# Edge attributes copied into tables ordered by source bucket and summed there by one-hot products, in place of scatter-adds; node stage with merged weights

## The chip, the core and the metric

The kernel runs on one core of one Trainium2 chip. The core has five instruction queues that run side by side: TensorE (PE, with its weight loads shown as PEld), VectorE (DVE), ScalarE (ACT), GpSimd (POOL) and SyncE (SP). In this kernel SP issues plain DMA transfers, and POOL issues the indirect ones, whose row addresses lie in an SBUF tile. All transfers run on the core's 16 DMA engines. The metric is the device time of one execution in microseconds; lower is better.

## What is computed

Two graph layers over 6250 nodes of 128 features and 100,000 edges, sorted by destination `dst`; `src` is random.

```python
# layer 0
radial = gaussian_smearing(edge_weight)                       # 50 values per edge
h = silu(concat(x[src], x[dst], radial) @ Wm1 + bm1)
messages = silu(h @ Wm2 + bm2) @ Wm3 + bm3
out = segment_sum(messages, dst)
u = silu(concat(x, out) @ Wu1 + bu1) @ Wu2 + bu2
x = layernorm(x + silu(u @ Wi1 + bi1) @ Wi2 + bi2)
# layer 1
xt = logmap0(x); xs = xt[src]
att = sigmoid(concat(xs, xt[dst], edge_attr_128) @ att_w.T + att_b)
agg = segment_sum(xs * att, src)
mean_src = segment_sum(edge_attr_128, src) / max(count(src), 1)
mean_dst = segment_sum(edge_attr_128, dst) / max(count(dst), 1)
x = layernorm(x + proj(expmap0(xt + agg + mean_src + mean_dst)))
```

The change is about `segment_sum(edge_attr_128, src)`: 100,000 rows of 512 bytes summed into 6250 rows in a random order.

## The kernel before

Edges are taken in 98 groups of 1024 (the last has 672). A group is 4 windows of 256 edges; a window holds 2 edges per partition, so a group has 8 blocks of 128 edges, numbered b = 0 to 7. Nodes are taken in 49 blocks of 128, so a node is a high part (block) and a low part (partition).

**Start.** Node projections x @ Wm1 (source half and destination half) are written to the DRAM tables `p_src` and `p_dst`; index tiles are built: `src_i`, `hif` and `lof` (high and low parts), `rel` (destination within its window's 64 nodes). Transposed x goes to DRAM as `x_t`.

**Edge loop** (lines 1058 to 1086, 98 + 2 passes of two halves). The order on every engine is that of the program. Per group: POOL gathers 8 blocks of `p_src` rows two groups ahead (`gather`, line 932, into `ga`); SP loads the broadcast source numbers `rows_all` (line 902) and destination numbers and distances `near`, the attributes `attr`, and 4 slices of `p_dst` (`load_rows`). PE forms layer 1 (`pa`, lines 999 and 1002: transposes of `ga`, features times `lw`), layer 2 (`pb`) and the sums over destinations with one-hots (`ps`, lines 1032 to 1036); ACT does the silu. DVE adds `ps` into the SBUF accumulator `acc` (line 1048). DVE also makes the target row of each edge: `seen` (line 948) compares the block's 128 sources with each other and counts equal ones before each edge; that `rank` times the table height plus the node's row is `to_i` (line 966). So two edges of one block never have the same target row.

**The scatter-adds** (line 868). Each block's 128 attribute rows go from SBUF to a DRAM table by an indirect DMA with add. There are three tables `t_src`, each of three layers (`RK`) for equal sources in one block, used in turn, since a scatter must wait for the one before it in its table. They are filled with zeros early in the edge loop (line 1070). From group 3 on, blocks 0 and 1 go in the edge loop. All other blocks wait: `scatter_late` loads three windows again (`attr_late`, four buffers) and scatters 6 blocks. 18 such portions are called in the node stage, 74 in the attention loop, the rest behind it.

**Node stage** (lines 1149 to 1189), 13 batches of up to 4 node blocks: xT is read back from `x_t`; `acc` holds the transposed message sums, attribute sums and counts; PE forms `po` = Wm3 part, `pu` = Wu1 parts, `pv` = Wu2, `pw` = Wi1, `py` = Wi2 plus bias plus x. Then a layernorm over all blocks (line 1140) and three reductions (lines 1200 and 1201), and the small steps of logmap0.

**Attention loop** (lines 1243 to 1281), one pass a group. SP loads `los` (low parts of source and destination, broadcast to all partitions); DVE makes the one-hots `ohT` (line 1249), `hi`, `lo` (line 1261, one for each of 8 blocks); PE looks up the two logit parts with 48 products (`pg`, line 1269), DVE picks and reduces (lines 1272, 1273), ACT takes the sigmoid; PE sums weights and counts by source with `lo` and `at` (`pS`, line 1281). SP and POOL run in program order here: each pass calls `scatter_late` ahead of its los loads.

**Closing stage** (from line 1290): the nine table layers are loaded in 7 parts and added (line 1321), divided by counts, added to `sup`, then expmap0, proj, the last layernorm and the output.

A flag `bad` is computed on the way; if an input does not fit the windows or the layers, a slower general path runs afterwards.

Of the kernel before, what the change touches and what calls it, by code (L numbers as in the profile page):

```python
# [16 lines left out]
P = 128  # L17
# [507 lines left out]

W = 64
WE = 256
RK = 3
NT = 3
NOW = 1  # L530

N_NODE, N_ATT = 18, 74

LAG = 3

# [41 lines left out]
def window_path(ctx, tc, bad, x, src, dst, edge_attr, edge_weight, Wm1, bm1, Wm2, bm2, Wm3, bm3,  # L577
# [8 lines left out]
    RROWS = ROWS + P  # L586
# [19 lines left out]
    t_src = [dram.tile([RK * RROWS, F], F32, name=f"t_src{i}") for i in range(NT)]  # L606
    x_t = dram.tile([F, NB, P], F32, name="x_t")
# [10 lines left out]
    nc.vector.tensor_scalar(dump, part, float(RK * RROWS - P), None, op0=OP.add)  # L618
# [13 lines left out]
    before = const.tile([P, P], BF16, name="before")  # L632
    nc.vector.tensor_scalar(before, cols, part, None, op0=OP.is_lt)
# [66 lines left out]
    bm3r = row(bm3, "bm3r")  # L700
    bi2r = row(bi2, "bi2r")
# [8 lines left out]
    src_i = keep.tile([P, 8, NG], I32, name="src_i")  # L710
    src_f = keep.tile([P, 8, NG], F32, name="src_f")
    row_f = keep.tile([P, 8, NG], F32, name="row_f")
    rel = keep.tile([P, 8, NG], F32, name="rel")
# [3 lines left out]
    rank_max = keep.tile([P, 8], F32, name="rank_max")  # L717
    ew3 = keep.tile([P, 8, NG], F32, name="ew3")
    nodeid = keep.tile([P, 4, NG], F32, name="nodeid")
# [3 lines left out]
    nc.vector.memset(rank_max, 0.0)  # L723
# [3 lines left out]
    zrow = const.tile([P, 5 * F], F32, name="zrow")  # L727
    nc.vector.memset(zrow, 0.0)

    def fills(t):  # L730

        return [(t[r * RROWS:r * RROWS + ROWS].rearrange("(p i r) f -> i p (r f)", p=P, i=10)[i], zrow)
                for r in range(RK) for i in range(10)]

    with tc.tile_pool(name="init", bufs=1) as init, \
            tc.tile_pool(name="initx", bufs=7) as initx, \
# [7 lines left out]
        for lo in range(0, NB, 7):  # L744
            hi = min(lo + 7, NB)
            x_sb = initx.tile([P, 7, F], F32, name="x_sb")
            full = min(hi, NFULL) - lo
            if hi > NFULL:
                nc.vector.memset(x_sb[:, NFULL - lo], 0.0)
            nc.sync.dma_start(x_sb[:, :full],  # L750
                              x[lo * P:(lo + full) * P].rearrange("(b p) f -> p b f", p=P))
            if hi > NFULL:
                nc.sync.dma_start(x_sb[:NREM, NFULL - lo], x[NFULL * P:])
            x_sbs.append(x_sb)
# [10 lines left out]
        for lo in range(0, NB, 7):  # L765
            hi = min(lo + 7, NB)
            x_sb = x_sbs[lo // 7]
            for b0 in range(lo, hi, 4):
# [6 lines left out]
                nc.scalar.dma_start(x_t[:, b0:b0 + nb], xT[:, :nb])  # L775
# [52 lines left out]
        nc.vector.tensor_copy(src_f, src_i)  # L828
# [7 lines left out]
        nc.vector.tensor_scalar(row_f, lof, float(ROWS // P), None, op0=OP.mult)  # L836
        nc.vector.tensor_add(row_f, row_f, hif[:, 0])
# [7 lines left out]
        b3 = split3(init, bm2x, [P, F], "bm2s")  # L845
        pick3 = init.tile([P, F], F32, name="pick3")
        sum3 = init.tile([P, F], F32, name="sum3")
        for i in range(3):
            is_i = init.tile([P, 1], F32, name=f"is{i}")
            nc.vector.tensor_scalar(is_i, part, float(i), None, op0=OP.is_equal)  # L850
            nc.vector.tensor_scalar(pick3 if i else sum3, b3[i], is_i, None, op0=OP.mult)
            if i:
                nc.vector.tensor_add(sum3, sum3, pick3)
        nc.vector.tensor_copy(bm2p, sum3[:, None].to_broadcast([P, 4, F]))

        nc.vector.memset(acc, 0.0)

    n_scatter = 0  # L860

    def scatter(g, b, rows_):
        nonlocal n_scatter
        t = t_src[0]
        if b >= 2 * NOW or g < LAG:
            n_scatter += 1
            t = t_src[n_scatter % NT]
        nc.gpsimd.indirect_dma_start(  # L868
            out=t[:, :], out_offset=bass.IndirectOffsetOnAxis(ap=to_i[:, b, g:g + 1], axis=0),
            in_=rows_, in_offset=None, compute_op=OP.add)  # L870
# [5 lines left out]
    with tc.tile_pool(name="eload", bufs=2) as eload, \  # L876
            tc.tile_pool(name="eattr", bufs=3) as eattr, \
# [4 lines left out]
            tc.tile_pool(name="ep3", bufs=2, space=PSUM) as ep3, \  # L882
            tc.manual_schedule():
        gas, attrs, ids, feats, hots, hid1, hid2, sums = ({} for _ in range(8))
# [7 lines left out]
        def load(g):  # L892
            nk, nf, ne = extent(g)
            e0 = g * GE
            rows = eload.tile([P, GE], I32, name="rows_all")
            near = eload.tile([P, GE], F32, name="near")
            near_i = near.bitcast(I32)
            if nf < nk:
                nc.vector.memset(rows, -1)
                nc.vector.memset(near_i[:KR], -1)  # L900
                nc.vector.memset(near[KR:], 0.0)
            nc.sync.dma_start(rows[:, :ne], src[e0:e0 + ne].partition_broadcast(P))
            nc.sync.dma_start(near_i[:KR, :ne], dst[e0:e0 + ne].partition_broadcast(KR))
            nc.sync.dma_start(near[KR:, :ne], edge_weight[e0:e0 + ne].partition_broadcast(KR))
            ids[g] = rows, near

        def load_attr(g):
            nk, nf, ne = extent(g)
            e0 = g * GE
            attr = eattr.tile([P, 4, 2, F], F32, name="attr")  # L910
            if nf < nk:
                nc.vector.memset(attr[:, nf], 0.0)
                nc.sync.dma_start(attr[:LP, nf],
                                  edge_attr[e0 + nf * WE:e0 + ne].rearrange("(p c) f -> p c f", c=2))
            nc.sync.dma_start(attr[:, :nf], edge_attr[e0:e0 + nf * WE].rearrange(
                "(k p c) f -> p k c f", k=nf, c=2))
# [19 lines left out]
        def prepare(g, half):  # L936

            nk = windows(g)
            rows, near = ids[g]
            if half == 0:  # L940
                feats[g] = (ework.tile([P, 4, 2, P], F32, name="feat"),
                            ework.tile([P, 8], F32, name="rank"))
            feat, rank = feats[g]

            seen = ework.tile([P, P], BF16, name="seen", bufs=1)
            by_block = rows.rearrange("p (k j c) -> p k c j", k=4, c=2)
            for b in range(4 * half, min(4 * half + 4, 2 * nk)):
                nc.vector.scalar_tensor_tensor(  # L948
                    seen, by_block[:, b // 2, b % 2], src_f[:, b, g:g + 1], before,
                    op0=OP.is_equal, op1=OP.mult, accum_out=rank[:, b:b + 1])  # L950
# [6 lines left out]
            if half == 0:  # L957
# [3 lines left out]
            to = ework.tile([P, 8], F32, name="to")  # L961
            nc.vector.tensor_tensor(rank_max[:, :2 * nk], rank_max[:, :2 * nk], rank[:, :2 * nk],
                                    op=OP.max)
            nc.vector.scalar_tensor_tensor(to[:, :2 * nk], rank[:, :2 * nk], float(RROWS),
                                           row_f[:, :2 * nk, g], op0=OP.mult, op1=OP.add)
            nc.vector.tensor_scalar(to_i[:, :2 * nk, g], to[:, :2 * nk], dump, None, op0=OP.min)
            del ids[g]

# [12 lines left out]
        def weigh(g):  # L981
            n = 2 * windows(g)
            prod = ework.tile([P, 8, F], F32, name="prod", bufs=1)
            nc.vector.tensor_mul(prod[:, :n], attrs[g].rearrange("p k c f -> p (k c) f")[:, :n],
                                 attw[:, 2:3].to_broadcast([P, n, F]))
# [7 lines left out]
        def layer1(i):  # L993
# [7 lines left out]
            for k in range(kk):  # L1001
                nc.tensor.matmul(pa[:, 2 * k:2 * k + 2], lhsT=lws[(4 * g + k0 + k) % NL],  # L1002
                                 rhs=feats[g][0][:, k0 + k], start=False, stop=k == kk - 1)
# [16 lines left out]
        def sum_up(i):  # L1020
# [5 lines left out]
            at_b = attrs[g].rearrange("p k c f -> p (k c) f")  # L1026
            ps = ep3.tile([P, 2, 3, W], F32, name="ps")
            for k in range(kk):
                for c in range(2):
# [4 lines left out]
                    nc.tensor.matmul(ps[:, k, 1], lhsT=at_b[:, b], rhs=hot[:, b],  # L1034
# [15 lines left out]
        clear = [f for t in t_src for f in fills(t)]  # L1050
# [6 lines left out]
        prepare(0, 0)  # L1057
        prepare(0, 1)
        for g in range(NG + 2):
            for half in range(2):  # L1060
# [7 lines left out]
                n_clear = 30 * RK // 3 // (2 * LAG) if g < LAG else 1  # L1068
# [4 lines left out]
                if LAG <= g < NG:  # L1073
                    for b in range(NOW * half, NOW * half + NOW):
                        scatter(g, b, attrs[g][:, b // 2, b % 2])
# [5 lines left out]
                if g + 1 < NG:  # L1081
                    prepare(g + 1, half)
                if g < NG and half == 1:
# [312 lines left out]
```

## Time and profile before

| What | us |
|---|---|
| 12 runs: median (lowest to highest) | 2935.99 (2920.3 to 2958.59) |
| profiled execution: its time | 2931.21 |
| its span on the core | 2929.4 |

| Engine | busy us | share of the span |
|---|---|---|
| POOL | 2058.7 | 70% |
| DVE | 1804.5 | 62% |
| PE | 1675.4 | 57% |
| PE weight loads | 1393.0 | 48% |
| ACT | 923.1 | 32% |

The mean granted PE clock was 0.705 of full speed. The DMA engines read 344.78 MB from HBM and wrote 94.11 MB. A busy share is a mean over stages that differ; the stages are told apart by their lines in the trace: `ga` runs only in the edge loop, `pu` and `pw` in the node stage, `pg` in the attention loop, `fb` in the closing stage.

### The profile page before, as it was taken

How to read it: one execution, taken by the hardware profiler on the slowest of the kernel's cores; microseconds unless marked ns; L12 is line 12 of the kernel's file. 1: busy time of each engine (PE TensorE's matmuls, PEld its weight loads, DVE VectorE, ACT ScalarE, POOL GpSimd, SP SyncE). 2: the span in 40 equal slices, each digit the busy share in tenths (PEclk: the TensorE clock that was granted, in tenths of full speed). 3: DMA queues.
4: the chain of work that ended last, by engine and by line, in shares of the span. 5: the costliest groups of instructions: out<-in, count | busy, mean ns of one | idle time of the engine just before them, and what ended most of it. 6: DMA issues, size and time to landing. Idle time of an engine off the chain costs nothing. (4 is left out here: it accounts for less than half of the span.)

```text
span 2929.4 us, 42152 instructions
## 1 busy us (share of the span) xinstructions
PE 1675.4 (57%) x13478; PEld 1393.0 (48%) x13478; DVE 1804.5 (62%) x5965; ACT 923.1 (32%) x1330; POOL 2058.7 (70%) x1590
## 2 busy tenths in 40 slices
PE   3677777776777787777776791454443444431000
PEld 2566666666666676666663451443332333331000
DVE  5565556565565655555551128998776777773267
ACT  1455555555555555555540000111000000100013
POOL 1567777777777777777777881777777777878810
PEclk8788888888888888898887786555555555555555
DMA  5987777766666676666655550676666666665484
GB/s 158 280 253 199 205 202 192 203 172 161 161 163 162 164 168 163 163 156 167 156 144 74 87 87 9 139 149 117 122 123 124 122 123 123 128 121 99 49 280 168
DMA packets 371430, 441.86 MB, mean 151 GB/s; under 512 B 46375, under 2 KB 285916, under 8 KB 371200
## 3 DMA queue, kind: packets, MB, share of 16 engines
q1 hardware_dynamic: 230216, 331.18, 37.9%
q0 software_dynamic: 138208, 103.35, 26.1%
q10 hardware_dynamic: 2776, 4.55, 0.4%
q8 instruction: 110, 1.80, 0.3%
q14 instruction: 120, 0.98, 0.1%
HBM read 344.78 MB, written 94.11 MB: 150 GB/s over the span
## 5 line engine op out<-in xcount | busy, mean ns | idle before, releaser
L868 POOL DMA_INDIRECT t_src<-attr_late,to_i x592 | 949.9, 1605 | 299.5 <-issue 159.7
L932 POOL DMA_INDIRECT ga<-p_src,src_i x782 | 787.1, 1006 | 314.8 <-issue 217.7
L1269 PE MATMUL pg<-a,ohT 128*128 128x49 bf16 x4692 | 213.4, 219 | 466.5 <-DVE ohT L1249 402.5
L1048 DVE TENSOR_TENSOR acc<-acc,ps 128x192 f32 x391 | 138.7, 355 | 542.0 <-PE ps L1036 500.9
L1269 PEld LDWEIGHTS <-ohT 128*128 128x128 bf16 x4692 | 200.4, 120 | 502.6 <-DVE ohT L1249 437.9
L999 PE MATMUL pa<-ident,ga 128*128 128x128 f32 x782 | 198.3, 335 | 345.6 <-DMA ga<-p_src,src_i 325.6
L868 POOL DMA_INDIRECT t_src<-attr,to_i x190 | 311.1, 1637 | 119.8 <-issue 66.4
L1032 PE MATMUL ps<-hot,h 128*128 128x64 f32 x1564 | 320.0, 288 | 1.4 <-ACT h L1018 1.4
L1034 PE MATMUL ps<-hot,attr 128*128 128x64 f32 x1564 | 311.6, 282 | 0.0
L999 PEld LDWEIGHTS pa<-ident,ga 128*128 128x128 f32 x782 | 105.8, 150 | 404.6 <-DMA ga<-p_src,src_i 228.6
L948 DVE SCALAR_TENSOR_TENSOR seen<-rows_all,src_f,before 128x128 bf16<-128x128 int32 x782 | 275.2, 352 | 36.1 <-DMA rows_all<-in_src_dram 12.6
L1005 ACT ACTIVATE h<-pa,bm1c 128x512 f32<-128x512 f32 x196 | 134.5, 686 | 508.9 <-PE pa L1002 508.7
L1016 PEld LDWEIGHTS pb<-wm,h 128*128 128x128 f32 x1564 | 268.4, 242 | 47.5 <-issue 23.5
L1002 PE MATMUL pa<-feat,lw 128*128 128x256 f32 x782 | 275.2, 489 | 8.2 <-DMA lw<-p_dst 8.1
L1276 ACT ACTIVATE lg<-lg,attb 128x8 f32<-128x8 f32 x98 | 29.5, 301 | 791.4 <-DVE lg L1275 791.4
L1016 PE MATMUL pb<-wm,h 128*128 128x128 f32 x1564 | 260.7, 322 | 0.0
L1032 PEld LDWEIGHTS ps<-hot,h 128*128 128x128 f32 x1564 | 251.6, 202 | 1.6 <-ACT h L1005 1.6
L1034 PEld LDWEIGHTS ps<-hot,attr 128*128 128x128 f32 x1564 | 247.6, 200 | 0.0
L1281 PE MATMUL pS<-at,lo 128*128 128x196 bf16 x782 | 145.1, 366 | 153.2 <-DVE at L1278 153.2
L1249 DVE TENSOR_SCALAR ohT<-los,part 128x2048 bf16<-128x2048 bf16 x98 | 76.2, 777 | 207.1 <-DMA los<-row_lo 207.1
L1002 PEld LDWEIGHTS pa<-feat,lw 128*128 128x128 f32 x782 | 174.1, 246 | 29.1 <-issue 8.8
L1281 PEld LDWEIGHTS <-lo 128*128 128x128 bf16 x782 | 101.0, 140 | 174.2 <-DVE at L1278 167.0
(225 smaller groups left out, 3216.8 us busy)
## 6 DMA issues: line engine op xcount, KB each, us to landing
los<-row_lo SPq DMA_DIRECT2D x196, 256.0 KB
rows_all<-in_src_dram SPq DMA_DIRECT2D x97, 512.0 KB
attr<-in_edge_attr_dram SPq DMA_DIRECT2D x97, 512.0 KB
attr_late<-in_edge_attr_dram SPq DMA_DIRECT2D x97, 384.0 KB
t_src<-zrow SPq DMA_DIRECT2D x90, 320.0 KB
fb<-t_src SPq DMA_DIRECT2D x56, 448.0 KB
near<-in_dst_dram SPq DMA_DIRECT2D x97, 256.0 KB
near<-in_edge_weight_dram SPq DMA_DIRECT2D x97, 256.0 KB
```

The source lines that it names most:

```text
L868: nc.gpsimd.indirect_dma_start(out=t[:, :], out_offset=bass.IndirectOffsetOnAxis(ap=to_i[:, b, g:g + 1], axis=0), in_=rows_, in_offset=Non ...
L932: nc.gpsimd.indirect_dma_start(out=gas[g][:, b], out_offset=None, in_=p_src[:, :], in_offset=bass.IndirectOffsetOnAxis(ap=src_i[:, b, g:g ...
L948: nc.vector.scalar_tensor_tensor(seen, by_block[:, b // 2, b % 2], src_f[:, b, g:g + 1], before, op0=OP.is_equal, op1=OP.mult, accum_out=r ...
L999: nc.tensor.matmul(pa[:, j], lhsT=gas[g][:, 2 * k0 + j], rhs=ident, is_transpose=True, start=j == 0, stop=False)
L1002: nc.tensor.matmul(pa[:, 2 * k:2 * k + 2], lhsT=lws[(4 * g + k0 + k) % NL], rhs=feats[g][0][:, k0 + k], start=False, stop=k == kk - 1)
L1005: nc.scalar.activation(hid1[i][:, :2 * kk], pa[:, :2 * kk], AF.Silu, bias=bm1c)
L1016: nc.tensor.matmul(pb[:, j], lhsT=h1[:, j], rhs=wm2, start=False, stop=j == nb - 1)
L1032: nc.tensor.matmul(ps[:, k, 0], lhsT=h2[:, 2 * k + c], rhs=hot[:, b], start=k == 0 and c == 0, stop=False)
L1034: nc.tensor.matmul(ps[:, k, 1], lhsT=at_b[:, b], rhs=hot[:, b], start=False, stop=False)
L1048: nc.vector.tensor_add(acc[:, :, bass.ds(at, W)], acc[:, :, bass.ds(at, W)], ps[:, k])
L1269: nc.tensor.matmul(pg[:, i, s], lhsT=ohT[:, s, b0 + i], rhs=a3[q][:, s], start=q == 0, stop=q == 2)
L1281: nc.tensor.matmul(pS, lhsT=lo[:, b], rhs=at[:, b], start=g == 0 and b == 0, stop=g == NG - 1 and b == n - 1)
```

## The change

The attribute rows are no longer added in DRAM. They are copied, without add, into tables in which each node block (bucket) owns a run of `cap` rows, and each edge gets a row of its own there. A row has 132 numbers instead of 128: the attributes, a one (for the count), the edge's attention weight (for blocks 3 to 7), and the low part of the source. Later each bucket's rows are loaded again, a one-hot is made of the low parts, and one product sums attributes, counts and weights of the 128 nodes.

- There are 14 tables: one lane for each of blocks 0 to 3, each split at group 70; one lane for blocks 4 and 5 and one for 6 and 7, each split at groups 35 and 70. Caps are 256 or 128 rows a bucket. Rows from a floor (`lo`) up to the cap are zeroed early in the edge loop, in 116 transfers.
- The row within the bucket comes from running counts. `rank` (PE, seven bf16 products with a triangle `tri` and `ones_b`) and `place` (DVE) take the place of `seen` and the `rows_all` load. Counts over a cap or under a floor set the flag of the general path.
- Blocks 0 and 1 still go in the edge loop from group 3 on. All blocks 2 and the six left of groups 0 to 2 go in the node stage, in 27 batches of up to 4 scatters with one load each into four buffers `r_tiles`; all blocks 2 of groups 0 to 69 go to one table, those of 70 to 97 to a second. Blocks 3 to 7 go in the attention loop, 5 a group, with their weight.
- Node stage: Wm3 Wu1b and Wu2 Wi1 are multiplied once at the start (`w3u`, `w2i`), which drops `po` and `pv` and their copies from each batch; x is loaded again and transposed, not read from `x_t`. The layernorm statistics and the two dot products are taken batch by batch, and the scaling of x is done on ACT inside the attention loop.
- Attention loop: software-pipelined by hand with los loaded three groups ahead, all engines in program order; `lo` and `at` only for blocks 0 to 2; each pass also sums one unit of buckets: 9 products (first 49 passes), 8, or 12.
- Closing stage: the last generation of lanes 3, 4/5 and 6/7 is summed in 28 units, and expmap0, layernorm and output run in 7 parts.

```diff
-RK = 3
-NT = 3
-NOW = 1
-N_NODE, N_ATT = 18, 74
+RW = 132
+EARLY, MIDDLE, LATE = (0, 1), (2,), (3, 4, 5, 6, 7)
 LAG = 3
+CUT1, CUT2 = 35, 70
+LANES = [((b,), ((0, CUT2, 256, 96), (CUT2, None, 128, 28))) for b in range(4)] + \
+    [((b, b + 1), ((0, CUT1, 256, 96), (CUT1, CUT2, 256, 96), (CUT2, None, 256, 76))) for b in (4, 6)]
...
     def scatter(g, b, rows_):
-        nonlocal n_scatter
-        t = t_src[0]
-        if b >= 2 * NOW or g < LAG:
-            n_scatter += 1
-            t = t_src[n_scatter % NT]
+        t, _ = table_of(g, b)
         nc.gpsimd.indirect_dma_start(
             out=t[:, :], out_offset=bass.IndirectOffsetOnAxis(ap=to_i[:, b, g:g + 1], axis=0),
-            in_=rows_, in_offset=None, compute_op=OP.add)
+            in_=rows_, in_offset=None)
...
-                nc.vector.scalar_tensor_tensor(
-                    seen, by_block[:, b // 2, b % 2], src_f[:, b, g:g + 1], before,
-                    op0=OP.is_equal, op1=OP.mult, accum_out=rank[:, b:b + 1])
+        def rank(g):
...
+            nc.tensor.matmul(part_(0, 0), lhsT=tri, rhs=hi[:, :4], start=True, stop=False)
+            nc.tensor.matmul(part_(0, 1), lhsT=ones_b, rhs=hi[:, :4], start=False, stop=True)
...
+        def place(g):
...
+            nc.vector.tensor_add(by_bank, counts, both(0))
+            nc.vector.tensor_add(counts, counts, both(1))
+            nc.vector.tensor_mul(prod, prod, his.pop(g))
+            slot = ework.tile([P, 8], F32, name="slot")
+            nc.vector.tensor_reduce(slot, prod, AX.X, OP.add)
...
+    middle = [[(g, b) for g in range(g0, min(g0 + 2, LAG)) for b in EARLY] for g0 in range(0, LAG, 2)]
+    middle += [[(g, b) for g in range(g0, min(g0 + 4, NG))] for b in MIDDLE for g0 in range(0, NG, 4)]
+    def move_middle():
...
+        for i, (g, b) in enumerate(bs):
+            nc.scalar.copy(t[:, i, F + 2:F + 3], lof[:, b, g:g + 1])
+        for i, (g, b) in enumerate(bs):
+            scatter(g, b, t[:, i])
...
+            nc.tensor.matmul(pu[:, :nb], lhsT=w3u, rhs=acc[:, 0, sl], start=True, stop=False)
+            nc.tensor.matmul(pu[:, :nb], lhsT=b3u, rhs=acc[:1, 2, sl], start=False, stop=False)
+            nc.tensor.matmul(pu[:, :nb], lhsT=wu1a, rhs=xT[:, :nb], start=False, stop=True)
...
+        def bucket_hot(unit, loaded):
...
+            for h in range(nh):
                 nc.vector.tensor_tensor(
+                    oh[:, h, :nj], cols[:, None, :].to_broadcast([P, nj, P]),
+                    bt[:, h, :nj, F + 2, None].to_broadcast([P, nj, P]), op=OP.is_equal)
+        def bucket_mm(unit, loaded, oh):
...
+                    nc.tensor.matmul(pb[:, h], lhsT=oh[:, h, j], rhs=bt[:, h, j, :S],
+                                     start=j == 0 and h == 0,
+                                     stop=j == nj - 1 and h == nh - 1)
...
+            def move(g):
+                t = rows_.pop(g)
+                for b in sorted(range(NE, 2 * windows(g)), key=lambda b: (b > 3 and b % 2, b)):
+                    scatter(g, b, t[:, b - NE])
...
+            for it in range(NG + 2):
...
+                one_hots(it + 1)
+                if it < NG:
+                    logits(it)
+                    move(it)
+                us = todo.get(it - 1, [])
+                pbs[it - 1] = [bucket_mm(u, l, o) for u, l, o in
+                               zip(us, loaded.pop(it - 1, []), ohs.pop(it - 1, []))]
+                look_up(it + 1)
+                if 0 < it <= NG:
+                    lo_at = weigh_one_hots(it - 1)
+                    sum_up(it - 1, *lo_at)
```

## The prediction

> **What bounds the kernel now.** I read first the busy times by stretch, cut where the chain of waits changes its line: start to first gather (77 us), edge loop (to 1546), node stage (to 1829), attention loop (to 2676), scatters left over (to 2797), closing stage. Columns: stretch, its length, busy us of PE, PEld, DVE, ACT, POOL, then the granted PE clock, DMA share, GB/s.
>
> ```profile
> 77.00:1546.00 1469.00, 1111.47 (x7289) 970.68 (x7287) 860.01 (x2964) 774.20 (x884) 1096.47 (x971) 0.85 0.71 181
> 1546.00:1829.00 283.00, 175.58 (x584) 96.43 (x583) 106.25 (x266) 20.26 (x30) 187.14 (x122) 0.72 0.44 66
> 1829.00:2676.00 847.00, 354.08 (x5424) 297.98 (x5424) 671.88 (x2342) 81.00 (x196) 661.74 (x413) 0.50 0.64 125
> 2676.00:2797.00 121.00, 4.85 (x52) 3.41 (x52) 23.09 (x90) 1.04 (x3) 102.32 (x60) 0.50 0.45 58
> 2797.00:2929.40 132.40, 0.00 (x0) 0.00 (x0) 105.75 (x241) 35.20 (x205) 0.35 (x1) 0.50 0.69 244
> ```
>
> No engine looks full, so next the costliest groups and the list of who waited for whom, for what the idle time is.
>
> ```profile
> L868 POOL DMA_INDIRECT t_src<-attr_late,to_i x592 | 949.9, 1605 | 299.5 <-issue 159.7
> L932 POOL DMA_INDIRECT ga<-p_src,src_i x782 | 787.1, 1006 | 314.8 <-issue 217.7
> L868 POOL DMA_INDIRECT t_src<-attr,to_i x190 | 311.1, 1637 | 119.8 <-issue 66.4
> ...
> PE pa L999 <- DMA ga<-p_src,src_i: 325.6, 209, 5.7
> ...
> DVE ohT L1249 <- DMA los<-row_lo: 207.1, 41, 38.2
> ...
> POOL t_src L868 <- DMA t_src<-attr_late,to_i: 74.8, 67, 2.8
> ```
>
> The idle time ahead of POOL's own instructions is mostly "issue": 0.30 us between any two of them (the timeline of POOL shows that gap at nearly every one). A group of the edge loop issues 8 gathers and 2 scatters: 8 x (1.006 + 0.30) + 2 x (1.637 + 0.30) = 14.3 us, and a group takes (1528 - 77) / 98 = 14.8 us (1528 is the start of the last gather). So POOL sets the edge loop, and PE waits 325.6 us for gathers. In the attention loop DVE waits for los, whose load stands in SP's queue behind attr_late loads that wait until scatters have freed a buffer: POOL starts 413 instructions in 847 us, one in 2.05, and some 60 more scatters at 1.55 + 0.30 fill the 121 us behind the loop. POOL bounds nearly everything up to 2797.
>
> Last, the chain of waits, for how long a scatter takes to land, counted from its start (two quiet ones, two under load):
>
> ```profile
> 1716.94 3.38 DMA t_src<-attr_late,to_i
> 2793.95 3.24 DMA t_src<-attr_late,to_i
> 2097.79 7.34 DMA t_src<-attr_late,to_i
> 2123.89 5.47 DMA t_src<-attr_late,to_i
> ```
>
> **The change part by part.** The sum is made against the profiled execution: 2931.2 us, 2929.4 of them span, 4.8 below the median shown (2936).
>
> *Scatter without add.* 782 scatters stay, of 528 instead of 512 bytes a row. No plain scatter is in the trace. Its POOL time lies between the indirect gather's 1.006 us (also 128 rows, one address a row, no add) and the adding scatter's 1.6; I take 1.0, since what it loses is the add and what it keeps is the gather's work turned round. Its landing: the quiet 3.3 us hold 1.55 us of POOL; with 1.0 instead, 2.7. With the 0.3 of issue the next dependent scatter starts 3.0 us after it; the far end is 3.3 + 0.3 = 3.6 quiet, and under load the chain's 5.5 and over.
>
> *Edge loop.* POOL per group falls to 8 x 1.31 + 2 x 1.30 = 13.1 us; gathers after one another show 0.95 in the timeline, so 12.6 at best. PE next: 1111 / 98 = 11.3 us busy now. Seven bf16 products of 98 or 196 columns are added for the rank; by the bf16 rows of 64 columns (195 ns) and 512 (495 ns) they are 0.22 to 0.28 us each, 1.8 us, and since PE's rows here overlap (the seven large groups make 1615 us against 1111 busy) 1.2 us on the path: 12.5. DVE: eight compares `seen` (0.352 us) with the small ones behind them go, one 392-wide compare, four 392-wide passes (0.55 each) and small ones come; 8.8 us a group before and after, covered. rows_all (512 KB a group) leaves SP's queue; one load for attr more and 116 fills instead of 90 enter it, under a DMA share of 0.71. I take 13.3 us a group, between 12.9 and, with the dear scatter, 14.4 (14.8 less the 38 us in which POOL's scatters and gathers waited for t_src). End of the gathers 77 + 98 x 13.3 = 1380, end of the loop 27 us behind it as now: 1407.
>
> *Middle scatters.* Here the change adds a wait. All blocks 2 go to one table (a second from group 70), so each of these 98 scatters waits until the one before it has landed; before, three tables took turns, and only 67 of 592 late ones waited. Queued behind the waiting scatter on POOL are all the others; behind the loads on SP, which wait for four buffers, stand xn and then los. 98 x 3.0 = 294, with six of blocks 0 and 1 and the first load 14 more: 308 us. Bounds: 98 x 2.65 (3.24 - 1.54 + 0.95, the issue gap running under the landing) and 98 x 3.6. The node stage's own work is hidden under it: now it ends with 54 us of layernorm and products (1774 to 1828) that move into the loop or to ACT, and two of its products a batch go; some 200 us remain. If the chain were short, these 200 would stand in its place.
>
> The Trainium skill, "DMA: Bandwidth & Descriptors", section "Anatomy of one DMA — SWDGE (gpsimd) path", speaks against such a chain: it fits 2.0 us + bytes / 436e3 to a transfer and puts most of it down to the write receipt, worst in HBM. For 67.6 KB my estimate from it is 2.2 us behind 1.0 of POOL, 3.5 with the issue; the total would be 50 us higher.
>
> *Attention loop.* Per group, 5 scatters: tables 3, 4, 5, 4, 5. Two dependent landings a group bound it: 2 x 3.0 = 6.0 quiet, 2 x 5.5 = 11 loaded. DVE: 671.9 / 98 = 6.86 us now; five compares `lo` (0.227 each by busy time) and 3 x 0.26 for the narrower `at` go: 4.95. Added is one one-hot of 1152 (the 1024-wide product costs 1.22, so 1.36), later 2 x 512 (0.69 each) or 2 x 768 (0.95), with an add of 0.43: 6.3 to 7.3. PE: 3.6 now, 2.7 without five sums; bucket products 9, 8 or 12 a group, at 0.43 us (the chain shows 0.42 for a 128x128 f32 pair in the node stage): 6.6, 6.1, 7.9. SP issues 12 DMAs instead of 3, some 5 us, covered. Three engines near 7 and a landing that varies: I take 7.9, with bounds 7.2 and 9.2, plus 10 us of ramp: 784.
>
> The clock rule of the page "TensorE: Matmul & The Clock Gate", Part 1, has the throttle let go when PE is busy; the rows agree (0.72 granted in the node stage, 0.50 here at 42% busy). By the rule the busier PE would leave 3.5 us a group; the sum is unchanged, since DVE and landings stay.
>
> *End.* The 121 us of scatters left over vanish: all are issued by the last group. Of the 132 us of closing, the 63 table loads and the 56 adds (61 us) go. Added are 28 units in 7 parts. DVE: 105.8 - 61 + 49 x 0.82 for one-hots 640 wide (between 0.69 for 512 and 0.95 for 768) + 28 x 0.4 for adds + 14 x 1.09 for two more passes a part + 14 for small steps done 7 times = 125. PE beside it: 245 x 0.43 = 105. With the sqrt, tanh, sqrt turns of the last part (3 x 1.28 of table loads and what they wait for), first load and output, 25: 150, bounds 135 (half of that covered) and 190 (the turns of all parts bare, 7 x 6 more).
>
> Sum: 1407 + 308 + 784 + 150 = 2649; with 2 us around the span 2651 in the profiled execution, 2655 beside the median.
>
> **The rivals.** *The plain scatter costs POOL as much as the adding one* (1.6). For: the same instruction with 128 addresses; against: the gather has these too. Edge 14.4 x 98 + 104 (77 ahead, 27 behind) = 1515, middle 98 x 3.6 + 14 = 367, attention 5 x 1.9 = 9.5 a group, 941, end 150: 2973 + 2, so 2975.
>
> *The landing takes the place of POOL.* Place: 98 middle scatters and 2 x 98 in the attention loop. With t from start to start the total is 1407 + 14 + 10 + 150 + 294 t + 2, above 2931 from t = 4.6 us. At 5.5, the loaded landing, it is 3200. For: the chain shows 5.5 to 7.3 there, and rows of 528 bytes lie off the old boundaries. Against: those rows are picked because they were late; one read of the old value falls away; scatters three apart (5.55 us) waited in one case of nine.
>
> *The edge loop gains nothing*, because PE, with the rank put in, or another wait keeps 14.6: 2655 + 98 x 1.3 = 2780.
>
> *The change doesn't do what it says*: with a bucket over its cap or under its floor the general path would run behind, and the time more than double. The inputs give 45 to 94 and 145 to 219 rows a bucket and table of one lane, 114 to 215 of two, within all bounds.
>
> **How the numbers follow.** Forecast 62%; edge loop without gain 15%; dear scatter 12%; landings 9%, of which over half lie above 4.6; general path 0.5%; the rest others. Predicted time 2655. Its own terms, each at the low end (12.9; 2.65; 7.2; 135), give 2500; 2900 takes in the second case, most of the attention loop at 9.2, and part of the first. What a measurement can't tell from no change is 0.3%, 9 us. Slower: the dear scatter nearly whole and most of the landings, 0.14; same 0.03; faster 0.83.
>
> **What would show it.** Right: POOL's scatter rows at 1.0 us; a group of the edge loop at 13.3; POOL in the middle idle between scatters with t_0_67 as releaser, 3.0 us from start to start; the attention loop with DVE over 80% busy at 7.9; nothing on POOL behind the last group. Wrong: scatter rows at 1.6; the middle over 400 us; an attention group over 9; a closing stage over 200.

## The result

| | median us | lowest to highest | runs |
|---|---|---|---|
| before | 2931.69 | 2917.86 to 2958.59 | 49 |
| after | 2963.0 | 2956.77 to 2970.62 | 12 |

The ratio is 1.0104, with a 95% interval of 1.0084 to 1.0123: the change costs 1%, where 2655 us was forecast, with 2900 as the far end of the range. The profiled execution of the changed kernel has a span of 2957.4 us. First its busy times by stretch, cut as those of before (stretch, length, busy us of PE, PEld, DVE, ACT, POOL, then granted PE clock, DMA share, GB/s): start to first gather, edge loop, node stage, attention loop, closing stage.

```profile
0.00:100.00 100.00, 40.76 (x179) 32.78 (x179) 50.77 (x113) 13.87 (x15) 11.26 (x26) 0.77 0.43 121
100.00:1395.00 1295.00, 1057.61 (x7944) 928.77 (x7942) 889.77 (x2207) 767.87 (x993) 975.69 (x974) 0.91 0.68 182
1395.00:1725.00 330.00, 101.87 (x488) 59.47 (x487) 76.09 (x243) 43.55 (x140) 102.40 (x105) 0.63 0.19 57
1725.00:2795.00 1070.00, 575.18 (x6623) 539.99 (x6623) 703.30 (x1993) 82.32 (x381) 501.81 (x474) 0.70 0.56 165
2795.00:2957.00 162.00, 90.11 (x621) 86.94 (x621) 130.96 (x426) 55.53 (x236) 12.08 (x11) 0.74 0.44 128
```

The edge loop is shorter: from the start of the first gather to the end of the last it takes 1279 us instead of 1438 (the 1469 of the stretch above begin before the first gather). The 121 us of scatters left over are gone. The attention loop, which now holds all its scatters, has grown from 847 to 1070, the node stage from 283 to 330. The last scatter ends at 2814.1, so 19 us of the last stretch still belong to the loop; behind it stand 143 us, where it was 132. In the attention loop no engine is near full: DVE 703 of 1070, PE 575, POOL 502. So the loop waits. The list of who waited for whom (engine and line, what it waited for: us in total, times, longest), over the whole span:

```profile
ACT attr L1466 <- DMA t<-attr,to_i: 793.4, 74, 30.5
PE pS L1530 <- DVE at L1524: 434.2, 96, 8.4
...
DVE lg L704 <- ACT att L1510: 327.7, 90, 5.9
...
ACT attr_last L1466 <- DMA t<-attr_last,to_i: 237.4, 23, 12.7
POOL t L927 <- ACT att L1510: 215.0, 89, 4.3
...
POOL t L927 <- DMA t<-attr,to_i: 203.0, 119, 4.2
```

Idle time of ACT alone would cost nothing. But here the three other engines wait in turn: PE for DVE, DVE for ACT's sigmoid (L1510), POOL for the same sigmoid, and ACT for landings of scatters ahead of L1466. The chain of waits of the changed kernel over one group (start, us, what) shows that this is a ring, a chain of waits in which each step waits for the one before it and the first for the last. (A scatter has landed when what waits for its data or its buffer may go on; the time of a landing is counted from the scatter's start on POOL.)

```profile
2270.18 0.30 ACT attr L1508
2270.48 0.19 ACT att L1510
...
2270.75 0.30 POOL t L927
2271.05 0.97 issue
2272.03 4.81 DMA t<-attr,to_i
...
2277.10 0.43 POOL t L927
2277.53 0.84 issue
2278.37 2.40 DMA t<-attr,to_i
...
2280.87 0.04 ACT attr L1466
...
2280.97 0.30 ACT attr L1508
```

Two sigmoids (L1508, L1510) free the group's five scatters. The second (block 4, 2272.03) lands 4.81 us later; block 5 goes to the same table and had to wait for it (2277.10). The last (block 7) lands 2.40 us after its start. Then ACT makes a 0.20 us copy (L1466) and the sigmoids of the next group: 10.8 us from sigmoid to sigmoid here, median 11.1 over the loop. L1466 writes the low parts of the group three ahead into the row buffer that the last group's scatters have just left (four buffers in turn), so it waits for their landing, and it stands in ACT's in-order queue ahead of the sigmoids of the present group.

One more fact is needed to read the runs below: in three of the five sets of runs PE was held back (granted clock 0.71 to 0.74 in the edge loop instead of 0.84 to 0.91), which lengthens the edge loop of every kernel, so times are compared within a set, or between sets in which PE was free.

### The profile page after: what moved, and what is told of

The parts are those of the page before. It is cut to its first block, busy times and chain, and to the rows that moved or that the text cites. A ratio compares the mean times of both kernels' runs of the same rounds, so it can differ in the third digit from the quotient of the medians.

```text
span 2957.4 us, 48129 instructions
## 1 busy us (share of the span) xinstructions
PE 1865.5 (63%) x15852; PEld 1647.9 (56%) x15852; DVE 1850.9 (63%) x4978; ACT 963.1 (33%) x1765; POOL 1603.2 (54%) x1590
## 5 line engine op out<-in xcount | busy, mean ns | idle before, releaser
L927 POOL DMA_INDIRECT t<-attr,to_i x448 | 467.5, 1044 | 623.3 <-DMA t<-attr,to_i 201.4
L1423 PE MATMUL pb<-acc,oh 128*128 128x130 f32 x2352 | 479.8, 390 | 116.1 <-issue 75.4
L1423 PEld LDWEIGHTS pb<-acc,oh 128*128 128x128 f32 x2352 | 456.0, 299 | 143.1 <-issue 103.3
L1493 PE MATMUL pg<-a,ohT 128*128 128x49 bf16 x4692 | 158.8, 194 | 218.6 <-DVE ohT L1473 206.3
L1530 PEld LDWEIGHTS <-lo 128*128 128x128 bf16 x294 | 30.5, 114 | 441.3 <-issue 432.4
L1466 ACT COPY attr<-lof 128x5 f32<-128x5 f32 x74 | 14.8, 200 | 793.4 <-DMA t<-attr,to_i 793.4
L704 DVE CAST lg<-att 128x3 bf16<-128x3 f32 x294 | 53.3, 181 | 334.4 <-ACT att L1510 327.7
L927 POOL DMA_INDIRECT t<-attr_last,to_i x144 | 150.7, 1046 | 185.2 <-DMA t<-attr_last,to_i 64.2
L927 POOL DMA_INDIRECT t<-attr_row,to_i x190 | 197.2, 1038 | 70.8 <-issue 49.4
L1139 PE MATMUL ps<-hot,attr 128*128 128x64 f32 x1172 | 227.8, 276 | 0.0
L1412 DVE TENSOR_TENSOR oh<-cols,acc 128x1152 f32<-128x1152 f32 (+3 forms) x196 | 180.9, 948 | 23.3 <-DMA acc<-t 23.3
```

The source lines that it names most:

```text
L927: nc.gpsimd.indirect_dma_start(out=t[:, :], out_offset=bass.IndirectOffsetOnAxis(ap=to_i[:, b, g:g + 1], axis=0), in_=rows_, in_offset=None)
L1139: nc.tensor.matmul(ps[:, k, 1], lhsT=head[:, b, :F] if b < 2 else rest[:, b - 2], rhs=hot[:, b], start=False, stop=False)
L1412: nc.vector.tensor_tensor(oh[:, h, :nj], cols[:, None, :].to_broadcast([P, nj, P]), bt[:, h, :nj, F + 2, None].to_broadcast([P, nj, P]), o ...
L1423: nc.tensor.matmul(pb[:, h], lhsT=oh[:, h, j], rhs=bt[:, h, j, :S], start=j == 0 and h == 0, stop=j == nj - 1 and h == nh - 1)
L1493: nc.tensor.matmul(pg[:, i, s], lhsT=ohT[:, s, b0 + i], rhs=a3[q][:, s], start=q == 0, stop=q == 2)
L1530: nc.tensor.matmul(pS, lhsT=lo[:, b], rhs=at[:, b], start=g == 0 and b == 0, stop=g == NG - 1 and b == NE - 1)
```

## The experiments

A "group" is the time from the first scatter of the attention loop to the end of the last, over 98. With PE held back the kernel before takes 3096 to 3135 us; with PE free 2931 to 2935. A set is a number of kernels run together with the kernel before (the expectations say "call"): first e1, e2, e3 and e4; then c0_after, f0, f1 and f2; then b0_before, r1, f4 and f3; then f0, f1, f2 and the kernel before again; last c0_after_c and f2. PE was held back in the first, second and fourth. The changed kernel itself, the control, ran in the second and the last.

### Controls: the changed kernel and the kernel before, as they are

> The changed kernel itself, as the control of this call, since chips differ (the one of the first call ran the kernel before in 3134 us, not in 2932). On a chip like the first: 2963, 10.9 us a group in the attention loop. On one like that of the first call: the edge loop 18.6 us a group, which no theory here speaks of, and 3440 to 3480.

> The changed kernel, as control. PE free (before near 2935): 2963, edge loop 13.0 us a group, attention 11.1. PE held back (before 3095 to 3135): 3480 to 3540, 18.5 and 11.1.

> The kernel before, as it is, for its trace on these chips, where it takes 3135 us instead of 2932 and the changed one 3537 instead of 2963. If the granted PE clock is what differs: the edge loop at a clock of 0.74 or less, PE with idle pieces that nothing ends, some 16.5 to 17 us a group instead of 14.55 (200 us in 98 groups), all other stages within 15 us of the first trace. If it is the transfers: the same clock as in the first trace, and longer landings in every stage.

> The kernel before. On a chip where it takes 2935: the trace of the first. On one where it takes 3135: the edge loop at a granted clock of 0.74 or less and 16.5 to 17 us a group, other stages unchanged, if the clock is the cause; longer landings everywhere, if the transfers are.

| run | PE | time us | edge loop, us a group | attention, us a group | behind the last scatter |
|---|---|---|---|---|---|
| c0_after | held back | 3536.5 | 18.4 | 11.1 | 143 |
| c0_after_c | free | 2967.6 | 13.1 | 11.1 | 143 |
| b0_before | free | 2940.4 | 14.7 | | 133 |
| b0_before_b | held back | 3113.3 | 16.5 | | 132 |

The attention loop does not care whether PE is held back; 11.1 belongs to the ring. The edge loop does, and the expectation of 16.5 to 17 for the kernel before held.

### Moving the copy

e1: the copy becomes `mark`, issued behind the sigmoids. e2: the copy stays, but rows are loaded two groups ahead, so that copy and load wait for the scatters of the group before last. f0 does both. In the expectations of the first set, theory A, where named, is the copy's ring; what its rivals expect stands beside it.

```diff
 # f0_copy (e1 has mark(it + 3) and load_late(it + 3); e2 changes load_late alone)
-                nc.scalar.copy(t[:, :n - NE, F + 2], lof[:, NE:n, g])
+            def mark(g):
+                if g < NG:
+                    nc.scalar.copy(rows_[g][:, :2 * windows(g) - NE, F + 2], lof[:, NE:2 * windows(g), g])
...
-                    load_late(it + 3)
+                load_late(it + 2)
...
                     logits(it)
+                    mark(it + 2)
                     move(it)
```

> Only the place of one small ACT copy in the attention loop changes: the copy that writes the low parts into the rows of group it+3 is issued behind the two sigmoids of group it instead of ahead of them. Theory A (the copy closes a loop: it waits until the scatters of group it-1 have landed, since they read the same buffer, and the sigmoid of group it, which the next scatters need, stands behind it on ACT): a group falls from 10.9 us to about 8.3, the time from 2963 to about 2710 (2660 to 2780). Theory B (two dependent landings a group on tables 4/5 and 6/7 bound the loop by themselves): a group stays above 10.5 us, 2920 to 2965. Theory C (PE with its bucket products bounds the loop): also unchanged.

> Rows are loaded and marked two groups ahead instead of three, with the same four buffers and the copy where it was, so the copy for group it+2 waits for the scatters of group it-2, not it-1. Theory A: the loop opens as in the run with the copy moved, 2690 to 2800. Theory B and C: unchanged, 2920 to 2965, or slower if the shorter look-ahead bares the loads.

> The copy of the low parts stands behind the sigmoids, and loads run two groups ahead instead of three, so that the copy waits for the scatters of two groups ago. The copy theory alone: the attention loop goes to the 7.9 us a group of the prediction, 290 us below the control. The theory of two dependent landings on one table alone: no gain, 10.9. Both: 8.9 to 9.4 a group, 150 to 200 below the control, with POOL waiting for its own landings.

> Copy behind the sigmoids alone. If PE was no limit to it on the other chip: 9.3 to 9.5 a group as there, and on a chip where before takes 2935, 2963 - 98 x 1.7 = 2795. If PE was: 8 to 8.5 a group, 2670 to 2720.

Measured, all with PE held back: e1 9.5 us a group (3360.6 us, ratio to before 1.0715, 1.0665 to 1.0765), e2 9.0 (3334.2; 1.0642, 1.0566 to 1.0719), f0 9.4 and in the repeat 9.3 (3348.5 and 3331.6). The times expected for e1 and e2 are for PE free, so there only the us a group compare. f0 lies 188 us below the control of its set. The ring through ACT is open: in the middle of the loop the sigmoid starts some 6 us ahead of its group's first scatter in e1 and e2 and 16 in f0 (medians), where in the changed kernel it starts 0.6 ahead. But the loop goes to 9.0 to 9.5, neither to the 8.3 that theory A expected of e1 nor to the 7.9 of the prediction: f0's reading "both". What holds it then, in the chain of waits of e1:

```profile
2608.10 0.98 POOL t L927
2609.09 0.33 issue
...
2609.65 5.27 DMA t<-attr,to_i
2614.92 0.27 issue
2615.18 0.96 POOL t L927
...
2618.59 5.56 DMA t<-attr,to_i
```

No ACT line is left in it: scatter, landing, next scatter of that table. In the repeat of f0 the median from the start of block 4 to that of block 5 is 4.0 us, from there to the next group's block 4 another 5.1: two dependent landings a group, 9.2 us from group to group. f0 was run with PE held back alone; since its sigmoids run far ahead of the scatters, PE is not what its scatters wait for.

### Another order, and four tables

e3 keeps the copy and turns the scatters from 3, 4, 6, 5, 7 to 4, 6, 3, 5, 7. f1 keeps the copy and gives blocks 4, 5, 6 and 7 a table each (128 rows a bucket, as many rows read back, and three products of `rank` fewer).

```diff
 # e3_order
-                for b in sorted(range(NE, 2 * windows(g)), key=lambda b: (b > 3 and b % 2, b)):
+                for b in sorted(range(NE, 2 * windows(g)), key=lambda b: (b % 2 and (1 if b == 3 else 2), b)):
 # f1_split
-    [((b, b + 1), ((0, CUT1, 256, 96), (CUT1, CUT2, 256, 96), (CUT2, None, 256, 76))) for b in (4, 6)]
+    [((b,), ((0, CUT1, 128, 48), (CUT1, CUT2, 128, 48), (CUT2, None, 128, 28))) for b in range(4, 8)]
```

> Only the order of the five scatters of a group changes, from blocks 3, 4, 6, 5, 7 to 4, 6, 3, 5, 7; the copy stays ahead of the sigmoid. Theory A: the first scatter of the pair on table 4/5 starts one issue (1.27 us) earlier in the closed loop, so a group falls by about 1.3 us: 2963 - 125 = 2840 (2810 to 2870). Theory B: two landings a group stay two landings a group, 2945 to 2970. Theory C: unchanged.

> Blocks 4, 5, 6 and 7 go to four tables instead of two, so that no scatter of a group waits for another of the same group; the rows read back stay as many. The copy theory alone: the loop sigmoid, five scatters, last landing, copy stays, 0.5 + 5 x 1.3 + 3 to 4 = 10 to 11 us a group, within 60 us of the control. The table theory alone: 7.9 a group, 290 us below.

> Four tables alone, the copy where it was: sigmoids, five scatters of 1.27, landing of the last, copy: 10.0 a group as there, 2963 - 98 x 1.1 = 2855. If PE held that run: 8 to 9 and 2660 to 2750.

e3: 10.0 a group (3420.5 us; 1.0914, 1.0867 to 1.0961). f1: 10.1 and 10.0 (3445.3, 91 below its control, and 3429.7). All three runs had PE held back. That is the copy's ring by itself, as expected for it (10 to 11 a group; the 91 us are more than the 60 expected). In f1 it is 5.9 us from the first to the last scatter and 4.1 from the last through landing, copy and sigmoid to the next group's first; in e3 6.0 and 3.8, where the changed kernel has 7.8 and 3.2: the two scatters on table 4/5, now three places apart, stretch the first part less.

### No loads of attributes in the attention loop

r1 leaves out the attribute loads of the attention loop, so old values are scattered.

```diff
-                nc.sync.dma_start(t[:, 0, :F], edge_attr[e0 + WE:e0 + 2 * WE].rearrange(
-                    "(p c) f -> p c f", c=2)[:, 1])
...
-                for k in range(2, nf):
-                    nc.sync.dma_start(t[:, 2 * k - NE:2 * k - NE + 2, :F],
-                                      edge_attr[e0 + k * WE:e0 + (k + 1) * WE].rearrange(
-                                          "(p c) f -> p c f", c=2))
```

> The changed kernel without the loads of edge attributes in the attention loop (one 128 KB and two 256 KB transfers a group; the rows scattered there hold old values), copy and tables as they are. If a loaded landing, slowed by these transfers in the same rings, is what lengthens the loop: landings near the quiet 1.9 to 2.4 us, a group at 7.4 to 8.4, DVE near full. If landings do not depend on them: within 0.5 of the control's 11.1.

2998.2 us and 11.5 a group (PE free), where the changed kernel took 2963.0 and 2967.6 in other sets: no gain, so the loads of attributes alone are not what makes the loop long. Its chain of waits:

```profile
2262.23 0.30 ACT attr_last L1503
2262.80 0.96 POOL t L927
...
2264.07 0.96 POOL t L927
...
2265.34 1.18 POOL t L927
...
2266.82 1.31 POOL t L927
...
2268.78 4.18 DMA t<-attr_last,to_i
2273.16 0.30 ACT attr L1503
```

Here the scatters hardly wait for tables: they follow each other in 1.27 to 2 us. The fifth then lands 4.18 us after its start instead of 2.40, and the ring is as long as before. What the table waits spread out in the changed kernel comes back in the last landing.

A short and a long landing differ in how busy the DMA engines were meanwhile. Three stretches, with columns as above (the DMA share is the last but one), are the landings of block 4 and block 7 in the changed kernel's chain and of the fifth scatter in r1's:

```profile
2272.03:2276.84 4.81, 4.30 (x47) 4.01 (x47) 4.78 (x11) 0.00 (x0) 2.36 (x2) 0.63 0.87 273
2278.37:2280.77 2.40, 0.00 (x0) 0.00 (x0) 0.00 (x0) 0.00 (x0) 0.97 (x1) 1.00 0.18 56
```

```profile
2268.78:2272.96 4.18, 2.77 (x54) 2.62 (x54) 1.28 (x6) 0.00 (x0) 0.96 (x1) 0.77 0.78 233
```

r1 still loads `los` and the bucket tables. The DMA packets of the two traces show the same over the whole loop. A scatter is 16 packets; in the order 3, 4, 6, 5, 7 the last of them ends 2.8, 3.7, 4.1, 2.5 and 1.9 us after the scatter's start in the changed kernel (medians), and 1.9, 1.9, 2.3, 4.3 and 4.1 in r1, where the loads that are left fall on other scatters. Where SP's loads kept the DMA engines under 10% busy (in the 2 us that begin 0.5 us after the start) it is 1.9 us in both kernels, at 80 to 95% 3.8 and 4.2. The packets themselves take no longer then (0.16 us each against 0.20). So a long landing goes with other loads in the way, not with the attributes' in particular; no run takes all of them away, so this is seen in the traces and not shown by an experiment.

### Both rings opened

f2 is f0 and f1 together, nothing else. It was run three times: f2_split_copy and f2_both_b with PE held back, f2_both_c with PE free.

> Both edits. If copy and tables close the loop together and each alone keeps a good part of it: 7.2 to 7.9 us a group, DVE over 85% busy there, 290 to 350 us below the control. If instead the loaded DMA rings or the PE clock hold the loop: over 8.5 a group, with DVE and POOL both below 75% busy.

> Both edits and nothing else. On a chip where PE runs free: DVE over 95% busy, 7.4 to 7.6 a group, 2963 - 98 x 3.6 = 2610. On one where it is held back: 9.2 a group and 3361 as before.

> Copy behind the sigmoids with loads two ahead, and four tables, nothing else. PE free: 7.4 to 7.6 us a group in the attention loop with DVE over 95% busy, node stage and closing as in the control, 98 x 3.6 = 350 below it, 2610; 2655 was the prediction. PE held back: 8.9 to 9.2 a group and 3320 to 3361 again.

With PE held back: 9.2 and 8.9 a group (3361.4 us, 175 below its control, and 3321.0), hardly better than f0. The timeline of the attention loop showed PE's look-ups there broken by idle pieces of 0.5 and 1.3 us that nothing ended, and DVE waiting for them. With PE free: **2614.7 us, ratio to before 0.8908 (0.8877 to 0.8939)**, 353 below the control of the same set (2967.6) and 5 from the 2610 expected; 7.6 a group. Its attention loop by stretch, and its waits between 1800 and 2400 us:

```profile
1725.00:2460.00 735.00, 492.11 (x6689) 466.19 (x6690) 704.89 (x2015) 83.16 (x386) 546.56 (x483) 0.81 0.85 242
```

```profile
ACT attr L1509 <- DVE lg L1508: 401.3, 60, 7.5
ACT attr_last L1509 <- DVE lg L1508: 134.1, 20, 7.5
...
POOL t L927 <- issue: 76.3, 250, 0.3
```

DVE is busy 705 of 735 us. ACT now waits for DVE alone, and 250 of POOL's waits are the plain 0.3 us between two of its instructions. The same DVE work (703 us) lay in the 1070 us of the changed kernel.

### Node stage: alternating tables; and the best version

e4 alternates the node stage's scatters between block 2's two tables (groups below and from 70); with that, each of them has a load of its own instead of one for up to four. f4 is e2, e3, e4 and the merged weights made behind the edge loop. f3 is f2, e4 and the same move of the merged weights.

```diff
 # e4_weave
-    middle += [[(g, b) for g in range(g0, min(g0 + 4, NG))] for b in MIDDLE for g0 in range(0, NG, 4)]
+    below, above = list(range(CUT2)), list(range(CUT2, NG))
+    while below or above:
+        n_ = 3 if len(middle) % 2 else 2
+        batch = below[:1] + above[:1] + below[1:n_]
+        del below[:n_], above[:1]
+        middle.append([(g, 2) for g in batch])
```

> Only the order of the scatters in the node stage changes: those of blocks 2 of groups 70 to 97 (second table) are put between those of groups 0 to 69 (first table). If the stage is a chain of landings on one table, 98 links of 3.1 us become 70: 28 x 3.1 = 87 us less, 2875 (2855 to 2900). If the node stage's own products, or ACT's marks between its silus, pace it: 2945 to 2975.

> Four edits on the two tables: loads two groups ahead, scatters in the order 4, 6, 3, 5, 7 (three apart on a table instead of two), scatters of the node stage alternating between the two tables of block 2, merged weights made behind the edge loop. The copy and the landings each gave part of 11.1 (8.9 with the first edit alone, 10.0 with the second alone): together 8.0 to 8.6 a group; node stage 75 us shorter; start of the gathers 20 us earlier. 350 to 420 below the control, 3120 to 3190. If DVE and a held-back PE are the floor already: 8.9 and 3210.

> Four tables for blocks 4 to 7, copy behind the sigmoids with loads two ahead, alternating tables in the node stage, merged weights behind the edge loop. No scatter of the attention loop waits for another of its group; if PE, held back in pieces of 0.5 and 1.25 us in the look-ups, bounds the loop as in the run before: 9.2 a group, 75 + 20 below it, about 3265. If POOL's waits were still the bound: 7.9 and 3140.

e4 (PE held back): 3453.5 us (1.1039, 1.0974 to 1.1104); from the first of its node-stage scatters to the last it takes 242 us, the other three kernels of that set 329 to 331, which is the 87 us expected, and the attention loop stays at 11.3. f4 (PE free): 2726.7, ratio 0.9274 (0.9231 to 0.9317), but 9.5 a group, not 8.0 to 8.6: in the order 4, 6, 3, 5, 7 block 5 stands three places behind block 4 instead of two, but the next group's 4 only two behind 5 instead of three; the two landings a group stay, 4.4 and 5.3 us from start to start. With the copy's ring open and PE free, this is what two tables in this order give. f3 (PE free): **2537.6 us, ratio 0.8635 (0.8596 to 0.8674)**, the fastest of all; both times expected (3265, 3140) were for PE held back. Its attention loop is f2's (7.6 a group). What it gains over f2 is the node stage, whose scatters take 255 us instead of 324 (the stage in f3, columns as above):

```profile
1400.00:1660.00 260.00, 119.64 (x510) 70.14 (x509) 78.04 (x250) 43.47 (x137) 101.61 (x104) 0.64 0.24 70
```

Making the merged weights later gained nothing at the start: the first gather starts at 100.1 us with them (changed kernel) and at 100.1 without (f3), where a DVE instruction of the start (`counts`) ends its wait.

## Why the prediction was wrong

The terms against the changed kernel's trace (first gather 100.1, last gather's end 1378.7, node-stage scatters from 1392.5 to 1716.8, attention scatters from 1720.5 to 2814.1, end 2957.4):

| term | forecast | measured |
|---|---|---|
| last gather ends | 1380 | 1378.7 |
| node-stage scatters | 98 x 3.0 + 14 = 308 | 324; median 3.04 from start to start |
| attention loop begins | 1407 + 308 = 1715 | 1720.5 |
| attention loop | 98 x 7.9 + 10 = 784 | 1094, 98 x 11.2 |
| behind it | 150 | 143 |

**Right.** POOL's price of a plain scatter, forecast 1.0, is 1.04:

```profile
L997 POOL DMA_INDIRECT ga<-p_src,src_i x782 | 776.6, 993 | 327.3 <-issue 201.4
L927 POOL DMA_INDIRECT t<-attr,to_i x448 | 467.5, 1044 | 623.3 <-DMA t<-attr,to_i 201.4
```

So the dear scatter (1.6) falls. The edge loop's end is right by two errors: 77 us was not the start of the first gather but POOL's idle time ahead of it. It started at 91.9 us before and at 100.1 after, and a group takes 13.05 instead of 13.3. The end of the node-stage scatters is right by luck as well: they begin at 1392.5 instead of 1407 and take 16 us longer, since 11 of the steps are over 3.6 us. The node stage's added wait is as forecast, one landing of a table between any two scatters; timeline of POOL in the changed kernel:

```profile
1486.05 0.97 POOL L927 DMA_INDIRECT t<-attr,to_i  x1 [2.36 <-DMA t<-attr,to_i]
1489.16 0.97 POOL L927 DMA_INDIRECT t<-attr,to_i  x1 [2.14 <-DMA t<-attr,to_i]
1492.20 0.97 POOL L927 DMA_INDIRECT t<-attr,to_i  x1 [2.07 <-ACT attr L1240]
```

From start to start it is 3.0 to 3.1 here, and 3.04 is the median of the stage. The Trainium skill, "DMA: Bandwidth & Descriptors", section "Anatomy of one DMA — SWDGE (gpsimd) path", gave an estimate of 3.5 by its fit; the measurement decides for 3.04.

DVE's price for an attention group, 6.3 to 7.3, is 7.3 in f2, and the closing stage 143 instead of 150.

**The step that failed** is the attention loop, "Three engines near 7 and a landing that varies: I take 7.9". All of the miss is there: 1094 - 784 = 310 us; without it the total would be 2647. Two things were wrong in it.

First, a wait was not seen. The working names the two landings on one table; it does not ask what else waits for the same landings. The copy of the low parts takes 0.20 us and looks free, but it waits for the row buffer, and behind it in ACT's queue stand the sigmoids that the next scatters need: the changed kernel's ACT waits 793 + 237 us at this copy (L1466). With the tables split and the copy kept (f1) this ring alone gives 10.0 to 10.1. Second, the landing was mis-sized. "2 x 3.0 = 6.0 quiet, 2 x 5.5 = 11 loaded" was there, and the value taken lies near the quiet end. With the copy out of the way and the tables kept (f0), two landings take 9.2: 4.6 each. Either fault alone breaks the range of 7.2 to 9.2 or stands at its end. They share the time: opening one ring earns 1.0 to 2.1 us a group (with PE held back), opening both 3.5 (with PE free), and then the forecast's own terms come out (2614.7 against 2655). Why a landing takes 2.4 us in one place and 4.8 in another is not shown by a run; in the traces it goes with how busy the DMA engines were (0.18 and 0.87 of the time in the two landings above).

**The rivals.** "The landing takes the place of POOL" named one of the two waits, at 9%, and its threshold of 4.6 us is what a landing measured in f0; but it was meant for both places, and in the node stage t is 3.04, and it did not see the copy. That the edge loop gains nothing is wrong with PE free (14.7 to 13.1) and right, and worse, with PE held back (16.5 to 18.4). Its reason, PE with the rank put in, would fit that; no run takes the rank out. The clock: PE's granted clock in the attention loop went from 0.50 to 0.70 as its busy share rose from 42% to 54%, and to 0.81 at 67% in f2. The Trainium skill, "TensorE: Matmul & The Clock Gate", Part 1, says that activity releases the throttle; these rows agree. The 3.5 us a group that the prediction worked out from it for PE were not reached: PE is busy 6.0 us a group in the changed kernel and 5.1 in f2.

## What to carry to other kernels

Where rows are built in a buffer and sent off, list every instruction that writes the buffer, however short, and ask what stands behind it in its engine's in-order queue: a 0.2 us copy that waits for a landing holds back whatever follows it. Count rings, not engines: follow a result from the instruction that makes it through the transfer, the buffer's release and the next write, and price it with the landing of that very stage, under the loads that run beside it. When two rings share a landing, removing one shows only part of the gain, so try both together before giving either up.

## What was not expected of the hardware

**PE held back.** The kernel before ran in 2935 us in one set of runs and in 3096 in the next on the same chip, so it is not the chip that decides. The granted clock in the edge loop was 0.84 and 0.74, while from the first scatter behind the node stage's to the last it took the same (1051 and 1050 us). For the changed kernel the same stretch of the edge loop, first with PE free (c0_after_c), then held back (c0_after):

```profile
500.00:1000.00 500.00, 406.27 (x3087) 355.49 (x3087) 342.28 (x841) 299.28 (x383) 383.91 (x381) 0.92 0.70 185
```

```profile
500.00:1000.00 500.00, 353.00 (x2167) 306.89 (x2165) 243.00 (x595) 210.79 (x267) 269.67 (x273) 0.75 0.56 150
```

2167 products instead of 3087 in 500 us. PE's timeline in the second has pieces like these, idle with nothing that ends them:

```profile
1001.59 0.23 PE L1141 MATMUL ps<-hot_b,ones_b 128*128 128x64 bf16 x1 [0.44 <-issue]
...
1003.01 0.26 PE L1139 MATMUL ps<-hot,attr 128*128 128x64 f32 x1 [0.71 <-issue]
1003.75 0.44 PE L1139 MATMUL ps<-hot,attr 128*128 128x64 f32 x1 [0.47 <-issue]
```

It costs the kernel before, whose edge loop POOL sets, about 170 us (1.7 a group) and the changed one, where PE stands next to POOL, some 525 (5.4 a group): the ratio of the two goes from 1.012 to 1.128 (1.1197 to 1.1364). What holds PE back, no run shows.

**Scatters.** An indirect scatter with add holds POOL for 1.6 us, the plain one for 1.04, the gather for 0.99. In the node stage, where the DMA engines are 19% busy, a plain scatter has the next one on its table 3.04 us behind it (median). Its landing took 2.4 us with the engines 18% busy in the attention loop, 4.2 and 4.8 at 78% and 87%.
